# One tap later: moving the offset product, the last stages, a load, statistics and filter sums in a deformable bottleneck

## The chip, the cores and the metric

The kernel runs on one core of a Trainium2 chip. Its engines are TensorE (PE for products, PEld for the loading of its weights), VectorE (DVE), ScalarE (ACT), GpSimd (POOL) and SyncE (SP, which here only issues DMAs); each has a queue of its own that it works through in order. The metric is the time of one execution in microseconds (us); lower is better.

## The reference

Two bottleneck layers follow each other on x of shape (4, 1024, 56, 56), in float32.

Layer 0 is a deformable bottleneck: `r = relu(conv1x1(x, w1))` to 256 channels; `off = conv3x3(r, w_off)` to 18 channels, a (dy, dx) for each of nine taps; for each tap and pixel r is sampled bilinearly at the displaced position (four corners, weighted, zero outside the image); the nine samples go through the 256 by 256 weights of their taps and a relu; then `x1 = relu(x + conv1x1(r2, w3))` with 1024 channels.

Layer 1 is an ordinary bottleneck with batch normalisation: conv1x1 to 256 channels (y1), bn and relu, conv3x3 (y2), bn and relu, conv1x1 back to 1024 channels, bn, a scale by softplus(residual_scale), and `relu(x1 + ...)`. Each bn needs mean and variance over all four images, so each convolution has to be finished before its normalisation can begin.

## The kernel before

An image has 3136 pixels. They are cut in seven blocks j = 0..6 of 448 pixels for the first stage, and in seven of 512, 512, 512, 512, 384, 384 and 320 for the later ones, so 28 blocks (n, j) in all. Layer 0 and the first convolution of layer 1 run in one long loop.

**Stage a** (`stage_a`, one block): the 1x1 convolution 1024 to 256 (products L317, relu L309), the transposes of its result (`ftp`, L370, in two PSUM banks) and their copies on ACT (`ft`, L377, L379, L380), from which four DMAs write the sampling table in HBM (L384, L388); then the product for the offsets (`pm`, L396, in a bank of the same pool of two), its copy on ACT (`part`, L405, one buffer) and six small DMAs to `offc` (L413). Inside it `stage_b` works out the positions of the block two before. x is loaded by `load_x` (L266), two blocks ahead for image 0, one block ahead for the others.

**Taps.** For each block and each of nine taps `sample` gathers four corners (POOL's indirect DMA L480; first corner on ACT L490, the others added on DVE L492), `turn` transposes the samples (`stp` on PE L517, in the same pool of two banks; `sts` copied on ACT L523, sums on DVE L525 to L527), and `tap` multiplies (PE L545; seven products as in Strassen's scheme). After tap 8 the partial products are copied (ACT L560 to L564), added (DVE L566 to L572) and go through the relu to `r` (ACT L574). `sample` runs two taps ahead of `tap`, and `turn` one.

**Stage c** (`stage_c`, one block): for each of eight parts of channels, x is copied to a bank of `psz` (`pr`, ACT L597; x loaded as `xr`, SP L590), the product with w3 is added (L601), relu to `x1t` (ACT L612), store (L613); these feed the first convolution of layer 1 (`acc3`, L627, banks of the same `psz`, of which there are two). At its end the sum is copied to `y` (ACT L637), `bn_stats` is taken of that copy (DVE L639), and the copy is stored (SP L640).

```python
                nc.scalar.copy(y1s[h], z)
                if part == 1:
                    nc.vector.bn_stats(y1_stats[:, h, b * 6 : b * 6 + 6], y1s[h])
                    nc.sync.dma_start(y1_v[n, :, h, blk], y1s[h])
```

**The order** is written by hand: the loop over taps (L789 to L837) gives the stages a budget of work after each tap and takes them forward with `next()`. What a stage yields is its cost. A `None` ends the stage's share for this tap, so that what follows it in the stage comes after the next tap. `last_ones` holds the blocks whose taps are done and for which stage c may begin. Image 0's stages a are run before the loop. `filters` (L673 and the lines after it) prepares the filters of the second convolution in between, from the last image's second block on.

**After the loop** come the scale and shift of bn1 (`scale_shift`, L840: `bn_aggr` on DVE, square root on ACT L128, four small operations on DVE); the second convolution in Winograd's form (normalisation on ACT L910, transformed inputs on DVE L940 to L959, products L993, filter sums `us` on DVE L1129, outputs and statistics in `end`, L1032 to L1080); bn2; a phase that forms the moments of the normalised y2 (relu L1238, mean row `first` L1248, transposes `tp` L1208, products L1227), from which bn3 is had without running the last convolution twice; and the last convolution with the residual (L1334 on).

Of the kernel before, what the change touches and what calls it, by code (L numbers as in the profile page):

```python
# [61 lines left out]
def deform_bottleneck_then_bn_bottleneck(  # L62
# [25 lines left out]
    x1_v = x1_d.rearrange("n (k p) q -> n p k q", p=128)  # L88
    u0_d = dram.tile([128, KB * 3 * CB], F32, tag="u0_d", name="u0_d")
# [11 lines left out]
    nc.sync.dma_start(ch, chan)  # L101
# [11 lines left out]
    y1_stats = const.tile([128, KB, NB * 6], F32, tag="y1_stats", name="y1_stats")  # L113

    y2_stats = const.tile([128, KB, 3 + 2 * 4 * 6], F32, tag="y2_stats", name="y2_stats")
# [26 lines left out]
    nc.sync.dma_start(s_t, res_scale.to_broadcast([128, 1]))  # L142
# [27 lines left out]
    with ExitStack() as l0:  # L170
# [16 lines left out]

        w1 = wa.tile([128, KC, CB], F32, tag="w1", name="w1")
# [66 lines left out]
        def load_x(n, j, kk):  # L255
            if n == N:
                return
            if (n, j) == (0, 0):
                nc.sync.dma_start(w1[:, kk : kk + 2], w1_v[:, kk : kk + 2])
            if n == 0:  # L260

                xt = gat.tile([128, 4 * CB], F32, tag="g", name=f"xt_{n}_{j}_{kk}")
                xt = xt[:, : 2 * BLK].rearrange("p (k q) -> p k q", k=2)
            else:
                xt = xin.tile([128, 2, BLK], F32, tag="xt", name=f"xt_{n}_{j}_{kk}")
            nc.sync.dma_start(xt, x_v[n, :, kk : kk + 2, j * BLK : (j + 1) * BLK])  # L266
            xts[n, j, kk] = xt
# [35 lines left out]
        def stage_a(n, j):  # L303
# [23 lines left out]
            if n == 0:  # L327

                sums = [
                    pst.tile([128, 512], F32, tag=f"tap{2 * (j % 2) + h}", name=f"acc1_{b}_{h}")[  # L330
                        :, :BLK
                    ]
                    for h in range(KB)
                ]
                for k in range(KC):
                    for h in range(KB):
                        product(h, k, sums[h], k == 0)
                    if k % 2 and j + 2 <= NJ:
                        load_x(*((0, j + 2) if j + 2 < NJ else (1, 0)), k - 1)
                    yield KB * BLK  # L340
                for h in range(KB):
                    clip(h, sums[h], col("a_b1", h))
            else:

                def channels(h):
                    z = psz.tile([128, 512], F32, tag="z", name=f"acc1_{b}_{h}")[:, :BLK]
                    begin_with(z, col("a_b1", h))
                    yield
                    for k in range(KC):
                        product(h, k, z, False)  # L350
                        if k % 2:
                            if h == KB - 1:
                                load_x(*following, k - 1)
                            yield 2 * BLK
                    clip(h, z, 0.0)

                yield from run([channels(h) for h in range(KB)])
# [24 lines left out]
            for corner, s in enumerate((0, PW)):  # L382
                r = q - s + TPAD
                nc.sync.dma_start(  # L384
                    tables[n][r : r + QFULL * 128, corner, :].rearrange("(t p) c -> p t c", p=128),
                    ft[:, :QFULL, :],
                )
                nc.sync.dma_start(  # L388
                    tables[n][r + QFULL * 128 : r + QB, corner, :], ft[:QREST, QFULL, :]
                )  # L390

# [187 lines left out]
        def stage_c(n, j):  # L579
# [35 lines left out]
            def first(h, part):  # L615
                z = psz.tile([128, 512], F32, tag="z", name=f"acc3_{b}_{h}_{part}")[:, :size]
                if part == 0:
                    y1s.append(
                        w3p.tile([128, 512], F32, tag="y1", name=f"y1_{b}_{h}", bufs=2)[:, :size]
                    )  # L620
                    begin_with(z, col("b1", h))
                else:
                    nc.scalar.copy(z, y1s[h])
                yield
                for i in range(KC // 2):
# [9 lines left out]
                    if i % 2:  # L635
                        yield 2 * size
                nc.scalar.copy(y1s[h], z)  # L637
                if part == 1:
                    nc.vector.bn_stats(y1_stats[:, h, b * 6 : b * 6 + 6], y1s[h])  # L639
                    nc.sync.dma_start(y1_v[n, :, h, blk], y1s[h])  # L640
# [9 lines left out]
            yield from run(jobs)  # L650

# [4 lines left out]
        def filters():  # L656
# [36 lines left out]
            nc.sync.dma_start(u0_d, w_0)  # L693
            yield
# [93 lines left out]
        stage, upcoming, extra, budget = None, None, None, 0.0  # L788
        for i, (n, j, k) in enumerate(taps):  # L789
# [6 lines left out]
            if k == TAPS - 1:  # L796
                last_ones.append((n, j))
# [47 lines left out]
    with l1:  # L845
# [187 lines left out]
        def end(i, p, q):  # L1033

            n, half = parts[i]
            even, odd = halves(i, p)
            if p in WIN:
# [15 lines left out]
            def stats(k):  # L1053
                if i in ENDS:
                    for o in range(KB):
                        at = 3 + (ENDS.index(i) * 4 + k) * 6
                        nc.vector.bn_stats(y2_stats[:, o, at : at + 6], r[k][:, o])
# [4 lines left out]
            elif p == 4:  # L1062
# [62 lines left out]
        for ps in ((1, 2), (3, 4), (0,), (5,)):  # L1125
            inputs(0, ds[0], ps)
            for p in ps:
                if p not in WIN:
                    nc.vector.tensor_add(us[p], u[p][:, :, 0], u[p][:, :, 1])  # L1129
                elif p not in EARLY:  # L1130
# [37 lines left out]
    def sums_of_filters():  # L1168
        nc.vector.tensor_add(c3s[:, 0], quarter[:, 1, 0], quarter[:, 1, 1])
        nc.vector.tensor_sub(c3s[:, 1], c3s[:, 0], quarter[:, 0, 0])  # L1170
        nc.vector.tensor_sub(c3s[:, 2], quarter[:, 0, 0], quarter[:, 1, 0])
        nc.vector.tensor_sub(c3s[:, 3], quarter[:, 0, 1], c3s[:, 1])
# [26 lines left out]
    with ExitStack() as l2:  # L1199
# [47 lines left out]
        for h in range(KB):  # L1247
            nc.tensor.matmul(  # L1248
                first[:, h * 128 : (h + 1) * 128],
                ref[:, h : h + 1].to_broadcast([128, 128]),  # L1250
                ident,
                start=True,
                stop=True,
            )
# [4 lines left out]
        for i in range(0, len(chunks), 2):  # L1259
# [4 lines left out]
            tp, yt = pixels(i)  # L1264
# [263 lines left out]
```

## Time and profile before

| what | us |
|---|---|
| median of 3 runs | 2837.42 (2833.97 to 2839.52) |
| profiled execution | 2845.98 |
| its span, first to last instruction | 2844.2 |
| PE busy | 2740.3 (96%) |
| DVE busy | 2141.3 (75%) |
| ACT busy | 1487.6 (52%) |
| POOL busy | 1216.8 (43%) |
| mean granted clock of TensorE | 0.989 |

By the timeline, image 0's stages a run to about 135 us, the loop over taps to 2109, the second convolution to 2423, the moments to 2555 and the last convolution to the end. On the page, "busy" is the time in which an engine works on an instruction; in an answer of the timeline each row has the start, the busy time, engine, line, operation, output and inputs, and in brackets the idle time of the engine just before it, with what ended it. "acc<-sts,w" is a product of `sts` with the weights w; the names leave buffer numbers out.

### The profile page before, as it was taken

The numbers are of one execution on the slowest core, as the hardware profiler recorded it, in microseconds if no ns is written. First come the engines' busy times: TensorE is split into PE (matmuls) and PEld (weight loads), VectorE is DVE, ScalarE is ACT, GpSimd is POOL, SyncE is SP. The second block draws the span as 40 slices with busy tenths as digits, with TensorE's granted clock in tenths as the row PEclk, the third lists the DMA queues.
The fourth block names the chain that finished last, engine by engine and source line by source line (L and its number), as shares of the span: only waits on it lengthen the run. The fifth ranks groups of instructions, "written<-read, shape, count | busy, mean of one in ns | idle before, by whom it ended". The sixth has DMA issues, their size and how long they took to land.

```text
span 2844.2 us, 39220 instructions
## 1 busy us (share of the span) xinstructions
PE 2740.3 (96%) x11901; PEld 1903.5 (67%) x11901; DVE 2141.3 (75%) x5069; ACT 1487.6 (52%) x3007; POOL 1216.8 (43%) x1050
## 2 busy tenths in 40 slices
PE   9979999999999999999999989999989999999999
PEld 4445566676666676667676657666769999875454
DVE  2287777888787888778778988778849987437777
ACT  2245554665655556555565656666652554514444
POOL 0065666466666556656555665554500000011211
PEclk9999999999999999999999999999999999999999
DMA  8598898999999998999998989999930110209998
GB/s 275 182 348 324 323 338 308 343 321 345 336 331 349 352 316 309 335 340 335 341 342 284 352 302 358 352 342 332 311 131 24 49 35 12 93 29 345 349 344 303
DMA packets 313029, 792.16 MB, mean 279 GB/s; under 512 B 33737, under 2 KB 134641, under 8 KB 312817
## 3 DMA queue, kind: packets, MB, share of 16 engines
q0 software_dynamic: 127296, 462.48, 45.6%
q1 hardware_dynamic: 167088, 275.78, 28.3%
q10 hardware_dynamic: 18432, 51.39, 4.6%
q8 instruction: 94, 1.54, 0.2%
q14 instruction: 119, 0.97, 0.1%
HBM read 640.68 MB, written 143.48 MB: 276 GB/s over the span
## 4 chain that ended last, share of the span: by engine, by line
PE 82%; DMA 8%; DVE 3%; ACT 3%; issue 2%; SPq 1%; another core or an unknown queue 1%; POOL 0%; ACTq 0%; POOLq 0%; DVEq 0%
PE acc L545 19%; PE pr L601 11%; PE acc L627 11%; PE acc L317 10%; PE q L993 8%; PE stp L517 6%; DMA g<-table,idxs 5%; PE u L1409 4%; PE c L1409 2%; PE v L1409 2%; PE acc_g L1227 2%; PE pm L396 2%; PE b L993 2%; DVE s L492 2%; PE tp L1208 1%
## 5 line engine op out<-in xcount | busy, mean ns | idle before, releaser
L480 POOL DMA_INDIRECT g<-table,idxs x900 | 1148.1, 1276 | 914.6 <-DVE s L492 259.6
L492 DVE SCALAR_TENSOR_TENSOR s<-g,wts,s 128x256 f32<-128x256 f32 (+1 forms) x2700 | 1173.2, 480 | 321.5 <-ACT s L490 176.7
L545 PE MATMUL acc<-sts,w 128*128 128x256 f32 (+2 forms) x3528 | 725.0, 355 | 5.9 <-ACT sts L523 4.3
L545 PEld LDWEIGHTS acc<-sts,w 128*128 128x128 f32 x3528 | 602.9, 191 | 55.3 <-ACT sts L523 6.6
L490 ACT ACTIVATE s<-g,wts 128x256 f32<-128x256 f32 x900 | 425.5, 511 | 245.5 <-PE stp L517 109.8
L601 PE MATMUL pr<-r,w 128*128 128x512 f32 (+2 forms) x896 | 369.8, 551 | 16.0 <-ACT pr L597 8.0
L317 PE MATMUL acc<-xt,w 128*128 128x448 f32 x896 | 358.4, 543 | 9.4 <-DMA xt<-in_x_dram 8.6
L627 PE MATMUL acc<-x1t,c1w 128*128 128x512 f32 (+2 forms) x896 | 357.4, 540 | 3.6 <-ACT x1t L612 1.7
L517 PEld LDWEIGHTS stp<-ident,s 128*128 128x128 f32 (+1 forms) x1800 | 211.6, 141 | 145.9 <-issue 92.5
L601 PEld LDWEIGHTS pr<-r,w 128*128 128x128 f32 x896 | 165.7, 192 | 165.1 <-issue 94.2
L517 PE MATMUL stp<-ident,s 128*128 128x128 f32 (+1 forms) x1800 | 253.6, 274 | 20.6 <-DVE s L492 10.4
L317 PEld LDWEIGHTS acc<-xt,w 128*128 128x128 f32 x896 | 166.9, 191 | 147.8 <-issue 142.5
L627 PEld LDWEIGHTS acc<-x1t,c1w 128*128 128x128 f32 x896 | 167.5, 190 | 143.2 <-issue 92.6
L523 ACT COPY sts<-stp 128x512 f32<-128x512 f32 (+2 forms) x504 | 242.9, 530 | 33.0 <-PE stp L517 26.1
L612 ACT ACTIVATE x1t<-pr,ch 128x512 f32<-128x512 f32 (+2 forms) x224 | 141.9, 633 | 141.5 <-PE pr L601 125.3
L1360 ACT ACTIVATE x1f<-x1f,sh_bn 128x896 f32<-128x896 f32 x112 | 116.0, 1041 | 150.4 <-DVE x1f L1357 121.8
L637 ACT COPY y<-acc 128x512 f32<-128x512 f32 (+2 forms) x112 | 59.5, 531 | 200.5 <-PE acc L627 182.5
L527 DVE TENSOR_TENSOR sts<-sts 128x512 f32<-128x512 f32 (+2 forms) x252 | 155.9, 619 | 0.7
L597 ACT COPY pr<-xr 128x512 f32<-128x512 f32 (+2 forms) x224 | 121.4, 542 | 4.1
L1357 DVE SCALAR_TENSOR_TENSOR x1f<-u,sc_bn,x1f 128x448 f32<-128x448 f32 x156 | 106.6, 684 | 18.9 <-PE u L1409 9.4
L993 PE MATMUL q<-v,u 128*128 128x196 f32 x576 | 109.6, 337 | 9.9 <-DVE v L945 8.7
L525 DVE TENSOR_TENSOR sts<-sts 128x256 f32<-128x256 f32 (+2 forms) x252 | 97.4, 387 | 25.4 <-ACT sts L523 21.3
(246 smaller groups left out, 2858.2 us busy)
## 6 DMA issues: line engine op xcount, KB each, us to landing
xt<-in_x_dram SPq DMA_DIRECT2D x112, 448.0 KB
x1f<-x_d SPq DMA_DIRECT2D x96, 448.0 KB
out_dram<-x1f ACTq DMA_DIRECT2D x96, 448.0 KB
xr<-in_x_dram SPq DMA_DIRECT2D x128, 256.0 KB
x_d<-x1t SPq DMA_DIRECT2D x128, 256.0 KB
table<-ft SPq DMA_DIRECT2D x56, 384.0 KB
g<-table,idxs POOLq DMA_INDIRECT x900
xr<-in_x_dram SPq DMA_DIRECT2D x64, 192.0 KB
```

The costliest lines, as they stand in the source:

```text
L317: nc.tensor.matmul(acc, w1[:, k, h * 128 : (h + 1) * 128], xts[n, j, k - k % 2][:, k % 2, :], start=start, stop=(k == KC - 1), skip_group_ ...
L480: nc.gpsimd.indirect_dma_start(out=g[:m], out_offset=None, in_=tables[n].rearrange("r q c -> r (q c)"), in_offset=bass.IndirectOffsetOnAxi ...
L490: nc.scalar.activation(s[:m], g[:m, 0:CB], AF.Copy, scale=wt[:, 0])
L492: nc.vector.scalar_tensor_tensor(s[:m], g[:m, corner * CB : (corner + 1) * CB], wt[:, corner], s[:m], ALU.mult, ALU.add,)
L517: nc.tensor.transpose(banks[h][:, t * 128 : t * 128 + m], s[:m, h * 128 : (h + 1) * 128], ident[:m, :m],)
L523: nc.scalar.copy(to, banks[h][:, :size].rearrange("p (e q) -> p e q", e=2))
L527: nc.vector.tensor_sub(sts[:, 5:7, :half], sts[:, 1:4:2, :half], sts[:, 0:2, :half])
L545: nc.tensor.matmul(sums[i], w2[:, a, k], sts[:, b, :half], start=(k == 0 and i % 2 == 0), stop=(k == TAPS - 1), skip_group_check=True,)
L601: nc.tensor.matmul(z, w3[:, h, k * 128 : (k + 1) * 128], r2[:, h, :size], start=False, stop=(h == KB - 1), skip_group_check=True,)
L627: nc.tensor.matmul(z, c1w[:, k, h * 128 : (h + 1) * 128], x1ts[k], start=False, stop=(i == KC // 2 - 1), skip_group_check=True,)
L993: nc.tensor.matmul(ps[:, o].rearrange("p r c -> p (r c)"), wt, x, start=first and j == 0 and (alone or o == 0), stop=last and j == len(pai ...
L1409: nc.tensor.matmul(to, wt, x, start=start, stop=stop, skip_group_check=True)
```

## The change

- The loads of `ch` and `s_t` are issued on ACT's queue instead of SP's.
- In `stage_a` a `yield None` stands ahead of the offset product, which then comes a tap later.
- A block enters `last_ones` one tap later than before (`done`).
- x block (1, 1) is loaded within stage a of (0, 6), into tiles of the pool of `r2` that are idle then.
- `bn_stats` of y1 reads the PSUM bank, ahead of the copy; y1 lies in tiles of another pool.
- `statistics` aggregates all blocks but the last ahead of the end; the last aggregate merges the result with the last block's (`y1_ends`).
- `filters` also forms three sums of filters (us1, us3, and us0, which is stored to HBM and loaded back).
- In the last part of the second convolution far_t is added to the halves before the last products (`closing`), statistics 1 and 2 come later, and the last statistics are of each half.
- The four sums of the last filters are formed on POOL instead of DVE.
- The mean row is multiplied between the first transposes of the moments phase.

```diff
-    nc.sync.dma_start(ch, chan)
+    nc.scalar.dma_start(ch, chan)
-    nc.sync.dma_start(s_t, res_scale.to_broadcast([128, 1]))
+    nc.scalar.dma_start(s_t, res_scale.to_broadcast([128, 1]))
+        y1_t = [wp.tile([128, 512], F32, tag=f"y1_{h}", name=f"y1_{h}") for h in range(KB)]
...
+            elif (n, j) == (1, 1):
+
+                xt = work.tile([128, KB, 512], F32, tag="r2", name=f"xt_{n}_{j}_{kk}", bufs=R2S)
+                xt = xt[:, :, :BLK]
...
-                    if k % 2 and j + 2 <= NJ:
-                        load_x(*((0, j + 2) if j + 2 < NJ else (1, 0)), k - 1)
+                    if k % 2:
+                        load_x(*((0, j + 2) if j + 2 < NJ else (1, j + 2 - NJ)), k - 1)
...
-                            if h == KB - 1:
+                            if h == KB - 1 and following != (1, 1):
...
+            yield None
+
             pm = ps1.tile([128, BLK], F32, tag="bank", name=f"pm_{b}")
...
-                    y1s.append(
-                        w3p.tile([128, 512], F32, tag="y1", name=f"y1_{b}_{h}", bufs=2)[:, :size]
-                    )
+                    y1s.append(y1_t[h][:, :size])
...
+                if part == 1:
+                    at = b * 6 if b < NB - 1 else 3
+                    to = y1_stats if b < NB - 1 else y1_ends
+                    nc.vector.bn_stats(to[:, h, at : at + 6], z)
                 nc.scalar.copy(y1s[h], z)
                 if part == 1:
-                    nc.vector.bn_stats(y1_stats[:, h, b * 6 : b * 6 + 6], y1s[h])
                     nc.sync.dma_start(y1_v[n, :, h, blk], y1s[h])
...
+        def statistics():
+
+            mv = const.tile([128, KB, 2], F32, tag="mv_y1", name="mv_y1")
+            count = float(N * HW - SIZES[-1])
+            for h in range(KB):
+                nc.vector.bn_aggr(mv[:, h, :], y1_stats[:, h])
+            nc.vector.memset(y1_ends[:, :, 0], count)
+            nc.vector.tensor_copy(y1_ends[:, :, 1], mv[:, :, 0])
+            nc.vector.tensor_scalar_mul(y1_ends[:, :, 2], mv[:, :, 1], count)
...
+            us_0 = w3p.tile([128, 512], F32, tag="x1t", name="us_0", bufs=X1S)
+            w_00 = w_0.rearrange("p (h j o) -> p h j o", h=KB, j=3)
+            nc.vector.tensor_add(
+                us_0.rearrange("p (h o) -> p h o", h=KB), w_00[:, :, 0], w_00[:, :, 1]
+            )
+            nc.sync.dma_start(us0_d, us_0)
...
+            for p in (1, 3):
+                us[p] = pool.tile([128, KB, CB], F32, tag=f"us{p}", name=f"us{p}")
+                nc.vector.tensor_add(us[p], u[p][:, :, 0], u[p][:, :, 1])
+                yield
...
             tap(n, j, k)
-            if k == TAPS - 1:
-                last_ones.append((n, j))
+            if done is not None:
+                last_ones.append(done)
+            done = (n, j) if k == TAPS - 1 else None
...
-            if extra and k in (1, 4, 7):
+            if extra and k in (1, 3, 5, 7):
...
+        last_ones.append(done)
         while last_ones or stage or upcoming:
             if stage is None:
+                if upcoming is None and len(last_ones) == 1:
+                    statistics()
...
+            if upcoming and not last_ones:
+                statistics()
...
-    sc1, sh1 = scale_shift(y1_stats, KB, cols("g1", KB), cols("be1", KB), "bn1")
+    sc1, sh1 = scale_shift(y1_ends, KB, cols("g1", KB), cols("be1", KB), "bn1")
...
+        nc.sync.dma_start(us[0], us0_d.rearrange("p (h o) -> p h o", h=KB))
...
+            closing = (i, p) == (len(parts) - 1, SEQ[-1])
+            if closing:
+                for to, c in ((odd, 1), (even, 0)):
+                    nc.vector.tensor_add(to, to, far_t[..., c:W:2])
...
-                stats(1)
-                stats(2)
+                if i == 0:
+                    stats(1)
+                    stats(2)
             elif p == 0:
                 nc.vector.tensor_add(r[0], r[0], sum_t)
                 stats(0)
+                if i:
+                    stats(1)
+                    stats(2)
+            elif closing:
+                stats(3, even)
+                stats(3, odd, 1)
...
-                if p not in WIN:
-                    nc.vector.tensor_add(us[p], u[p][:, :, 0], u[p][:, :, 1])
-                elif p not in EARLY:
+                if p in WIN and p not in EARLY:
...
-        nc.vector.tensor_add(c3s[:, 0], quarter[:, 1, 0], quarter[:, 1, 1])
+        nc.gpsimd.tensor_add(c3s[:, 0], quarter[:, 1, 0], quarter[:, 1, 1])
...
-        def pixels(i):
+        def pixels(i, between=None):
...
+                if c == 0 and between is not None:
+                    between()
...
-            tp, yt = pixels(i)
+            tp, yt = pixels(i, mean_row if i == 0 else None)
```

More of the change, by code (lines that the diff above doesn't have):

```diff
@@ L88, in deform_bottleneck_then_bn_bottleneck @@
     x1_v = x1_d.rearrange("n (k p) q -> n p k q", p=128)
+    us0_d = dram.tile([128, KB * CB], F32, tag="us0_d", name="us0_d")
     u0_d = dram.tile([128, KB * 3 * CB], F32, tag="u0_d", name="u0_d")
@@ L112, in deform_bottleneck_then_bn_bottleneck @@
     nc.vector.memset(eps_t, EPS)
-    y1_stats = const.tile([128, KB, NB * 6], F32, tag="y1_stats", name="y1_stats")
-    y2_stats = const.tile([128, KB, 3 + 2 * 4 * 6], F32, tag="y2_stats", name="y2_stats")
+    y1_stats = const.tile([128, KB, (NB - 1) * 6], F32, tag="y1_stats", name="y1_stats")
+    y1_ends = const.tile([128, KB, 3 + 6], F32, tag="y1_ends", name="y1_ends")
+    y2_stats = const.tile([128, KB, 3 + (2 * 4 + 1) * 6], F32, tag="y2_stats", name="y2_stats")
     def scale_shift(stats, k, g, be, name):
@@ L787, in deform_bottleneck_then_bn_bottleneck @@
         turn(*taps[0])
-        stage, upcoming, extra, budget = None, None, None, 0.0
+        stage, upcoming, extra, done, budget = None, None, None, None, 0.0
         for i, (n, j, k) in enumerate(taps):
@@ L1051, in end, with stats @@
             r = [rows_of(n, half, k) for k in range(4)]
-            def stats(k):
+            def stats(k, of=None, more=0):
                 if i in ENDS:
+                    of = r[k] if of is None else of
                     for o in range(KB):
-                        at = 3 + (ENDS.index(i) * 4 + k) * 6
-                        nc.vector.bn_stats(y2_stats[:, o, at : at + 6], r[k][:, o])
+                        at = 3 + (ENDS.index(i) * 4 + k + more) * 6
+                        nc.vector.bn_stats(y2_stats[:, o, at : at + 6], of[:, o])
             if p == 2:
@@ L1168, in sums_of_filters @@
     def sums_of_filters():
-        nc.vector.tensor_add(c3s[:, 0], quarter[:, 1, 0], quarter[:, 1, 1])
-        nc.vector.tensor_sub(c3s[:, 1], c3s[:, 0], quarter[:, 0, 0])
-        nc.vector.tensor_sub(c3s[:, 2], quarter[:, 0, 0], quarter[:, 1, 0])
-        nc.vector.tensor_sub(c3s[:, 3], quarter[:, 0, 1], c3s[:, 1])
+        nc.gpsimd.tensor_add(c3s[:, 0], quarter[:, 1, 0], quarter[:, 1, 1])
+        nc.gpsimd.tensor_sub(c3s[:, 1], c3s[:, 0], quarter[:, 0, 0])
+        nc.gpsimd.tensor_sub(c3s[:, 2], quarter[:, 0, 0], quarter[:, 1, 0])
+        nc.gpsimd.tensor_sub(c3s[:, 3], quarter[:, 0, 1], c3s[:, 1])
     def wide(n, j, k, name):
@@ L1246, in deform_bottleneck_then_bn_bottleneck, with mean_row @@
         first = ps1.tile([128, 512], F32, tag="bank", name="first")
[L1247 to L1254, printed above, removed]
+        def mean_row():
+            for h in range(KB):
+                nc.tensor.matmul(
+                    first[:, h * 128 : (h + 1) * 128],
+                    ref[:, h : h + 1].to_broadcast([128, 128]),
+                    ident,
+                    start=True,
+                    stop=True,
+                )
         relu(0, 128, BLK)
```

## The prediction

> **What bounds the kernel now.** I read the page's busy shares first, then the timeline of TensorE (PE) in stretches, its gaps, and what ScalarE (ACT), VectorE (DVE) and the DMA queues did in each.
>
> ```profile
> PE 2740.3 (96%) x11901; PEld 1903.5 (67%) x11901; DVE 2141.3 (75%) x5069; ACT 1487.6 (52%) x3007; POOL 1216.8 (43%) x1050
> ```
>
> TensorE is idle for 2844.2 − 2740.3 = 104 us only. The change removes no matmul, so what it can win is some of those 104 us, and the half-clock time behind them. In the record of the granted clock every gap of about 2 us and more is followed by 3.4, 6.8 or 10.2 us at 0.5; 6.8 us at half speed are 3.4 us of lost work. Three places matter. The first is stage c of block 2, on the timeline of PE and of ACT:
>
> ```profile
> 310.88 0.60 PE L545 MATMUL acc<-sts,w 128*128 128x256 f32 x2
> 316.32 2.93 PE L601 MATMUL pr<-r,w 128*128 128x512 f32 x3 [4.84 <-ACT r L574]
> ...
> 312.51 0.51 ACT L490 ACTIVATE s<-g,wts 128x256 f32<-128x256 f32 x1 [2.72 <-DMA g<-table,idxs]
> 315.56 1.32 ACT L574 ACTIVATE r<-r,ch 128x512 f32<-128x512 f32 x2
> ```
>
> The reader sees stage c's first product wait for the relu of r, which stands on ACT behind samples that wait for gathers. The second is the offset product, here of block 14:
>
> ```profile
> 696.39 1.04 PE L370 MATMUL ftp<-ident,feat 128*128 128x128 f32 x8
> 697.27 0.70 PE L601 MATMUL pr<-r,w 128*128 128x320 f32 x2
> 700.03 2.31 PE L396 MATMUL pm<-feat,woff 128*64 128x448 f32 x6 [2.06 <-ACT ft L377]
> ...
> 699.00 0.51 ACT L490 ACTIVATE s<-g,wts 128x256 f32<-128x256 f32 x1 [1.53 <-DMA g<-table,idxs]
> 699.41 0.57 ACT L377 COPY ft<-ftp 128x512 f32<-128x512 f32 x1
> ```
>
> Ten such gaps (1.00, 0.61, 0.42, 2.06, 1.31, 0.71, 0.38, 1.85, 0.93, 0.83) sum to 10.1 us. The third is the boundary to the second convolution, and its end:
>
> ```profile
> 2109.06 0.43 PE L627 MATMUL acc<-x1t,c1w 128*128 128x320 f32 x1
> 2109.59 0.43 ACT L637 COPY y<-acc 128x320 f32<-128x320 f32 x1 [1.78 <-PE acc L627]
> 2110.03 1.28 ACT L128 ACT_TABLE_LOAD   x1
> 2110.04 0.33 SPq L640 DMA_DIRECT2D y_d<-y  x1
> 2110.57 0.91 DVE L121 BATCH_NORM_AGGREGATE mv_bn<-y_stats 128x2 f32<-128x168 f32 x1
> 2112.70 4.12 ACT L910 ACTIVATE y<-rows,sh_bn,sc_bn 128x812 f32<-128x812 f32 x4 [0.88 <-DVE sh_bn L133]
> 2114.70 1.29 DVE L1129 TENSOR_TENSOR us<-u 128x512 f32<-128x512 f32 x2 [2.10 <-DMA y_d<-y]
> 2118.01 0.67 PE L993 MATMUL q<-v,u 128*128 128x196 f32 x1 [8.51 <-DVE v L945]
> ...
> 2421.14 1.63 PE L993 MATMUL q<-v,u 128*128 128x196 f32 x8 [0.59 <-ACT y L1031]
> 2425.37 0.61 DVE L121 BATCH_NORM_AGGREGATE mv_bn<-y_stats 128x2 f32<-128x51 f32 x2
> 2427.14 7.19 ACT L1238 ACTIVATE y<-y,sh_bn,sc_bn 128x128 f32<-128x128 f32 x12 [0.82 <-DVE sh_bn L133]
> 2428.77 1.20 PE L1248 MATMUL first<-ident,both 128*128 128x128 f32 x4 [6.00 <-issue]
> ```
>
> At the first, a chain of statistics; DVE waits until 2114.70 for the last store (4.6 us after issue). At the second, PE waits 6.00 us behind statistics, aggregate and first relu.
>
> **The Trainium skill.** "TensorE: Matmul & The Clock Gate", Part 1, gives half clock after an idle window of about 3.4 us; the trace agrees on the half, though gaps from 2 us can bring it. "PSUM — Partial Sum Buffer", bank collisions, has two engines on one bank ordered, two readers too. So in the new order the copy of z on ACT must wait for the statistics that DVE reads from z; before, the copy (0.43 to 0.59 us) went first and statistics read its result. The same page's section on engine and sequencer instructions says that ACT's and DVE's queues are strict FIFO: what stands behind a waiting copy waits too (the ft copy above did). "DMA: Bandwidth & Descriptors", anatomy of one DMA, puts about 2 us on a DMA's completion; here 4.6 us, and that is used.
>
> **The change part by part**, against the profiled execution (span 2844.2, time 2845.98 us; the median of the runs is 2837.42, 8.6 lower).
>
> *Two small loads to ACT's queue.* SP issued ch and s_t at 0.74 and 1.19, w at 1.65 us. The first product (6.45 us) waits for x; x moves up by 0.9 us, and PE is full until 104 us: −0.9.
>
> *Offset product a tap later.* The order of PE after the change has the transposes ftp, one or two products, then stp of the next tap, which needs the same two banks and so the same ft copy. Pm's 10.1 us do not vanish, they stand before stp. Taken 0; −10 if ACT's copies come earlier, +4 since stp loses pm's 2.5 us of cover for DVE's samples (blocks 17 and 24 had them 2.6 and 1.5 us after the copy). The part copy moves too: at 215.38 stp waited 5.45 us for it (then 6.8 at half clock, 8.9 in all), since the previous block's six offc DMAs filled its buffer. Both blocks shift alike and stp still follows: −1.5, between −8.9 and 0. Those offc DMAs pass to a later place of SP's queue, behind the tap's other loads and stores; their readers, the positions, run two blocks later and have tens of microseconds.
>
> *Stage c a tap later.* The products of one more tap stand before it, and the relu is done by then: 4.84 + 3.4 = 8.2 us at 311. Stage c's xr loads and x1 stores on SP shift with it, in step with their consumers. DVE's samples are late there as well, so −7 (0 if stp waits in its place). The same wait at 2087.82 (2.57) stays: the last tile's order is unchanged.
>
> *x block (1,1) ahead.* 1.8 MB go into image 0's stages, where PE is full and DMA half free; the 1.3 MB of xr that stood there go later. At 155.67 PE waited 2.14 us for this x, and in the stretch 137 to 235 PE is busy for 75.9 of 98 us while the DMA engines are at 0.92 and 335 GB/s. The net 0.5 MB less in that stretch is 1.5 us; the wait is 2.1 more. One may contain the other: −2.5, between −6 and +2 (xr late for stage c of block 0 after 240 us).
>
> *Statistics from PSUM.* 56 statistics of 0.48 to 0.71 us now stand between the last product and the copy. The bank comes free 0.8 to 1.2 us later (DVE's own work ahead included; 4 to 10 in four cases near 1118 to 1130 and 1672 to 1680). Of the two banks' slack, counted block by block in the trace before, two cases had 0.1 us or less, two 1.2 and 1.6, all others 2.3 or more. That is 1 to 3 us; ACT held behind adds little while it is at 52%. +2.5, between 0 and +25.
>
> *Boundary.* The early aggregate saves part of 0.91 us, but the square root cannot start before the table load ends at 2111.31 (it started at 2111.52). The two adds of 1.29 leave DVE. Against this y copy comes 0.5 us later, and y1's new place is memory that the normalised image takes: the first normalisation waits for the store, 2110.5 + 4.6 = 2115.2 instead of 2112.70. It then gives the first 1.03 us piece at 2116.2 and a second at 2117.3, where L940 began at 2115.91: +1, between −2 and +3, at half clock all the same.
>
> *Filters.* Three adds of 0.65 us on DVE, hidden in its 25% (the edges' adds before 2116 are what they replace), and 262 KB out and back, 0.8 us each at 340 GB/s. On SP the store stands ahead of the rows load, read only at the boundary some 400 us on, and the reload ahead of the u loads, which waited for the store's landing at 2114.69 in any case: +0.5; +3 if uncovered. The 5.24 us gap at 1647, DVE waiting on the end filters, stays.
>
> *End of the second convolution.* The two statistics moved off DVE before 2417 are replaced there by one subtraction of like length: the gap of 2.71 stays. After the last product DVE had 0.56 + 0.98 + 1.04 us to the aggregate; now 0.56 + 0.56 and four half statistics: −0.5. The transposes start with the first two relus, about 0.6 and 1.1 us after 2426.6, mean row between them: −1.2. The four sums on POOL free 2.7 us of DVE where PE waits 0.26 at most: 0; POOL's memsets behind them have three buffers of lead, +1 otherwise.
>
> Sum: −0.9 + 0 − 1.5 − 7 − 2.5 + 2.5 + 1 + 0.5 − 0.5 − 1.2 = −9.6. The profiled execution would be at 2836.4; a timed run at 2837.4 − 9.6 = 2827.8, say **2828**.
>
> **Rivals.** (A) The sum as above, 2818 to 2836; chance 0.50. (B) Pm's waits fall as well, since the ft copies lie ahead of the samples once the tap is re-spaced, and with them 215: −9.6 − 10.1 − 7.4 = −27, 2810; for it speaks that PE has no other work due in these gaps, against it the order; 0.20. (C) The gaps only move: stp waits at 311 for late samples, and x fills no gap: −9.6 + 7 + 2.5 = 0, some 2837; 0.15. (D) Slower: the copy's wait on DVE. ACT, FIFO, holds samples and sts copies behind each of 56 copies; with 0.45 us of each exposed, 25 us, in place of 2.5: −9.6 − 2.5 + 25 = +13, 2850. It decides past 0.32 us exposed a time (56 times that are 18 us, against −12.1, 5.7 above no change). For it: DVE has some 6.5 us of work in a tap of 7.3 and takes its samples from ACT. Against it: two banks with slack over 2 us. 0.15.
>
> **How the numbers follow.** 0.2% is 5.7 us, about what a measurement tells from no change. Faster (under 2831.7): 0.8 of A, all of B, a little of C: 0.62. Same: 0.2 of A, most of C: 0.23. Slower: D, 0.15. B's tail and the milder half of D give the range 2805 to 2845; A's own is 2818 to 2836.
>
> **What would show it.** Right: no gap at 311, first product near 5.5 us, ten small gaps now before stp with ft L385 as releaser, ACT's y copy released by DVE, the boundary gap at 9 to 10, the one at 2422 at about 4.5. Wrong: new ACT-bound gaps in the loop after stage c's ends; a pm group without waits and nothing in its place; a boundary under 8.

## The result, and the profile after

The changed kernel takes 2864.68 us (median of 8 runs, 2851.31 to 2880.35) where the kernel before takes 2838.47 in the same comparison (8 runs, 2832.65 to 2845.91): the ratio is 1.0092, 95% interval 1.0068 to 1.0117. That is 26 us slower. 2828 us and a gain were forecast. The two profiled executions lie closer together, their spans 21 us apart, so what the traces show below is somewhat less than the loss.

The page after, busy shares, then the costliest groups of PE that wait, with their idle time and its first releaser:

```profile
span 2865.3 us, 39151 instructions
...
PE 2754.3 (96%) x11901; PEld 1906.3 (67%) x11901; DVE 2139.3 (75%) x5073; ACT 1491.4 (52%) x3007; POOL 1227.5 (43%) x1054
...
L611 PE MATMUL pr<-r,w 128*128 128x512 f32 (+2 forms) x896 | 371.1, 556 | 20.4 <-ACT pr L607 13.3
L527 PE MATMUL stp<-ident,s 128*128 128x128 f32 (+1 forms) x1800 | 261.8, 275 | 39.8 <-ACT ft L385 14.7
```

The same two groups on the page of the kernel before:

```profile
L601 PE MATMUL pr<-r,w 128*128 128x512 f32 (+2 forms) x896 | 369.8, 551 | 16.0 <-ACT pr L597 8.0
L517 PE MATMUL stp<-ident,s 128*128 128x128 f32 (+1 forms) x1800 | 253.6, 274 | 20.6 <-DVE s L492 10.4
```

The number of matmuls is the same, 11901. PE's idle time went from 2844.2 − 2740.3 = 104 us to 2865.3 − 2754.3 = 111, and 14 us more are "busy": the time at half clock went from 67.2 to 79.9 us, which is some 6 of the 14, and the rest lies, it seems, in the steps between matmuls, which are pipelined with modelled ends, so that a short wait counts as busy. By stage, from the starts and ends of the same products in both traces (the first stretch ends at the start of PE's first gap of over 1 us after it has begun, 2.83 us before and 3.27 after, ahead of transposes of image 0):

| stretch | before, us | after, us | difference |
|---|---|---|---|
| start to that gap | 104.28 | 105.77 | +1.5 |
| from there to the end of the loop | 2005.2 | 2021.3 | +16.0 |
| boundary to the second convolution | 8.51 | 9.39 | +0.9 |
| second convolution | 304.8 | 306.9 | +2.2 |
| gap at its end | 6.00 | 4.42 | −1.6 |
| the rest, to the last product | 410.1 | 412.2 | +2.2 |

So most of the loss sits in the loop over taps. The 2.2 us of the second convolution and of the rest were not followed up. The waits of the loop, on the timeline of PE and of ACT; first at the place of the 4.84 us gap, then a wait of stp behind ftp:

```profile
309.25 3.60 PE L611 MATMUL pr<-r,w 128*128 128x512 f32 x8
317.00 3.78 PE L611 MATMUL pr<-r,w 128*128 128x512 f32 x4 [4.16 <-ACT pr L607]
...
313.82 0.51 ACT L500 ACTIVATE s<-g,wts 128x256 f32<-128x256 f32 x1 [2.83 <-DMA g<-table,idxs]
315.96 0.51 ACT L500 ACTIVATE s<-g,wts 128x256 f32<-128x256 f32 x1 [1.05 <-DMA g<-table,idxs]
316.37 0.58 ACT L607 COPY pr<-xr 128x512 f32<-128x512 f32 x1
...
880.87 1.04 PE L378 MATMUL ftp<-ident,feat 128*128 128x128 f32 x8
881.75 1.03 PE L555 MATMUL acc<-sts,w 128*128 128x256 f32 x4
885.14 0.55 PE L527 MATMUL stp<-ident,s 128*128 128x128 f32 x3 [2.36 <-ACT ft L385]
```

Stage c now starts without waiting for the relu, and stops four products later (each leaves two records, hence x8) for the copy of x: ACT is held by samples that wait for gathers either way. And stp waits for the copies of ft, as pm did before.

The boundary, and the end of the second convolution:

```profile
2127.05 0.50 DVE L648 BATCH_NORM_STATS2 y_ends<-acc 128x6 f32<-128x320 f32 x1 [1.42 <-PE acc L635]
2127.64 0.42 ACT L649 COPY y<-acc 128x320 f32<-128x320 f32 x1 [1.78 <-DVE y_ends L648]
2129.38 0.29 ACT L131 ACTIVATE sc_bn<-mv_bn,eps_t 128x2 f32<-128x2 f32 x1
2132.18 4.14 ACT L948 ACTIVATE y<-rows,sh_bn,sc_bn 128x812 f32<-128x812 f32 x4 [2.50 <-DMA y_d<-y]
2136.41 0.99 PE L1031 MATMUL q<-v,u 128*128 128x196 f32 x2 [9.39 <-issue]
...
2445.40 0.67 DVE L124 BATCH_NORM_AGGREGATE mv_bn<-y_stats 128x2 f32<-128x57 f32 x2
2447.76 1.41 PE L1256 MATMUL tp<-ident,y 128*128 128x128 f32 x3 [4.42 <-ACT y L1288]
```

Shift and scale are ready at 2130.46 (the last of their operations on DVE), 3.4 us after the last product, but the normalisation starts 1.7 us later, at 2132.18, released by the store of y, whose memory its result takes. In brackets is ACT's whole idle time, 2.50.

### The profile page after: what moved, and what is told of

Same layout as the page of the kernel before. It is cut to its first block, busy times and chain, and to the rows that moved or that the text cites. A ratio compares the mean times of both kernels' runs of the same rounds, so it can differ in the third digit from the quotient of the medians.

```text
span 2865.3 us, 39151 instructions
## 1 busy us (share of the span) xinstructions
PE 2754.3 (96%) x11901; PEld 1906.3 (67%) x11901; DVE 2139.3 (75%) x5073; ACT 1491.4 (52%) x3007; POOL 1227.5 (43%) x1054
## 4 chain that ended last, share of the span: by engine, by line
PE 63%; DMA 7%; DVE 4%; ACT 3%; issue 2%; ACTq 0%; SPq 0%; POOLq 0%; POOL 0%; DVEq 0%
PE acc L555 14%; PE pr L611 9%; PE acc L635 9%; PE q L1031 7%; PE acc L325 5%; PE stp L527 4%; DMA g<-table,idxs 4%; PE u L1462 3%; PE acc_g L1277 2%; PE c L1462 2%; PE b L1031 2%; PE v L1462 2%; DVE s L502 2%; DMA out_dram<-x1f 1%; PE pm L406 1%
## 5 line engine op out<-in xcount | busy, mean ns | idle before, releaser
L555 PE MATMUL acc<-sts,w 128*128 128x256 f32 (+2 forms) x3528 | 732.9, 356 | 1.2 <-issue 0.6
L527 PE MATMUL stp<-ident,s 128*128 128x128 f32 (+1 forms) x1800 | 261.8, 275 | 39.8 <-ACT ft L385 14.7
```

The source lines that it names most:

```text
L527: nc.tensor.transpose(banks[h][:, t * 128 : t * 128 + m], s[:m, h * 128 : (h + 1) * 128], ident[:m, :m],)
L555: nc.tensor.matmul(sums[i], w2[:, a, k], sts[:, b, :half], start=(k == 0 and i % 2 == 0), stop=(k == TAPS - 1), skip_group_check=True,)
```

## The experiments

A ratio is to the kernel before on the same chip, with its 95% interval. Kernels named together in one heading, unless it says otherwise, ran on one chip; across headings only the ratios compare. The intervals reach 0.001 to 0.003 to each side; a difference that they cover tells nothing.

### Undoing one of three parts, and all three

Three parts of the change act on the loop: the pause ahead of the offset product (P), stage c a tap later (C), the statistics read from PSUM ahead of the copy (B). Each is undone in the changed kernel.

`u_pm`, P undone:

```diff
-            yield None
-
             pm = ps1.tile([128, BLK], F32, tag="bank", name=f"pm_{b}")
```

> The changed kernel with the offset product back at its old place (no yield ahead of it), all else as changed. Theory P, the offset product: its wait went to stp and grew there (stp stalls +27 us, pm stalls -12 in the loop), so most of the loop's loss goes: 12 to 16 us faster than the changed kernel, ratio to before about 1.004. Theory B, the copy that waits for the statistics: this run stays near 1.009, within 4 us of the changed kernel. Theory C, the later stage c: the same, near 1.009.

`u_bn`, B undone:

```diff
+                nc.scalar.copy(y1s[h], z)
                 if part == 1:
...
-                    nc.vector.bn_stats(to[:, h, at : at + 6], z)
-                nc.scalar.copy(y1s[h], z)
+                    nc.vector.bn_stats(to[:, h, at : at + 6], y1s[h])
```

> The changed kernel with the statistics of y1 taken of the copy again, after it; all else as changed. Theory B: ACT waited 82 us for DVE in 27 of these copies, and this held the samples back; without it 10 to 15 us faster than the changed kernel, ratio to before about 1.004 to 1.005. Theory P or C: not over 3 us faster, near 1.008 to 1.009.

`u_c`, C undone for all blocks but the last:

```diff
-            if done is not None:
-                last_ones.append(done)
-            done = (n, j) if k == TAPS - 1 else None
+            if k == TAPS - 1 and i + 1 < len(taps):
+                last_ones.append((n, j))
```

> The changed kernel with a block's stage c free to begin right after its tap 8 again (for all blocks but the last, whose order is the same anyway). Theory C: the copies of x for stage c now meet the samples that wait for gathers (pr stalls of 4.2 us at 313 and 3.3 at 402); undone, 5 to 10 us faster than the changed kernel, ratio about 1.006. Theory P or B: within 3 us of the changed kernel, or slower by up to 8 us, since the gap of 4.84 us at 311 and its half clock come back.

`u_all3`, the three edits together:

> The changed kernel with all three of these undone: what is left is the early x block, the earlier loads, statistics(), the filter sums and the end of the second convolution. If the three carry the loss, this is 3 to 8 us faster than before (ratio 0.997 to 0.999). If it stays at 1.004 or more, the loss lies in the rest: the early x block or the queues it shifts.

| kernel | ratio | interval |
|---|---|---|
| changed | 1.0092 | 1.0068 to 1.0117 |
| u_pm | 1.0039 | 1.0026 to 1.0052 |
| u_bn | 1.0069 | 1.0050 to 1.0089 |
| u_c | 1.0050 | 1.0031 to 1.0069 |
| u_all3 | 0.9994 | 0.9978 to 1.0009 |

The three together carry the loss: 0.0098 of it, 28 us, go when they are undone. The rest of the change is worth nothing that these runs can tell, where 3 to 8 us had been expected. Undoing P gives 15 us; undoing C gives 12, where the theory P or B had expected 3 at most (the two intervals just touch); B's 6.5 us fit neither of its expectations, lie within the two intervals and show nothing yet.

### One part alone, and both transposes and product late

From `u_all3`, one part is put back. `r_pm` has P alone, `r_c` C alone, `r_bn` B alone. `r_both` moves the transposes a tap later too, so that pm follows ftp directly as before:

```diff
             yield None
+            yield None
 
             ft = worka.tile([128, QFULL + 1, CB], F32, tag="ft", name=f"ft_{b}")
```

> From the kernel with all three undone (ratio 0.9994), the offset product alone moved a tap later again. Theory P: it costs by itself what its undoing gave, 12 to 15 us (ratio 1.004 to 1.005). If the three need each other (a rival: each loss is only there in company), under 5 us, ratio below 1.001.

> As r_pm, but the transposes ftp are moved a tap later together with the offset product, so that pm still follows ftp directly and stp does not. Theory P in its narrow form (the loss comes from stp standing right behind ftp, in whose banks it waits for the copies of ft, not from lateness): ratio within 0.0015 of 0.9994. Rival, lateness of the stage itself: as r_pm, 1.004 or more.

> From the kernel with all three undone, stage c alone a tap later again. Theory C: 5 to 12 us slower than 0.9994, ratio 1.001 to 1.004. The forecast of the prediction (the gap of 4.84 us at 311 and its half clock go): 3 to 8 us faster, 0.997 to 0.998.

> From the kernel with all three undone, the statistics alone taken from PSUM ahead of the copy. Theory B: 4 to 8 us slower, ratio 1.001 to 1.002. If the undoing's 0.0023 was noise: within 2 us of 0.9994.

| kernel | ratio | interval |
|---|---|---|
| r_pm | 1.0034 | 1.0020 to 1.0049 |
| r_both | 1.0169 | 1.0144 to 1.0194 |
| r_c | 1.0009 | 0.9997 to 1.0022 |
| r_bn | 1.0002 | 0.9988 to 1.0017 |

P costs 0.0040, 11 us, alone. C alone costs 0.0015, some 4 us, with intervals that overlap, and B alone nothing that shows (2 us, where 4 to 8 had been expected). Alone the three make some 17 us by these figures, together 28: part of the loss seems to come only in company, the rival that `r_pm` was to tell from theory P. `r_both` felled the narrow theory: with pm directly behind ftp again it is not near 0.9994 but 50 us slower than `u_all3`, far beyond the 1.004 named for mere lateness, which it does not rule out. What waits for what (the list of waits by tile, with the sum in us and the number of waits: for stp in `r_pm`, then for pm in `u_all3`, then for pm in `r_both`) shows where the wait for the copies stands:

```profile
  DVE s L502: 12.1, 11
  ACT ft L385: 11.1, 7
```

```profile
  ACT ft L385: 10.8, 10
```

```profile
  ACT ft L386: 26.5, 15
```

The wait for the copies of ft is 11.1 us at stp in `r_pm` and 10.8 at pm in `u_all3`. There it moved and did not grow, and the 11 us that P costs must come on top, which the narrow theory does not explain. In `r_both` it grew, at its old place.

What `r_pm` and `r_both` have in common is the pause itself. A `None` ends the stage's share of this tap with its budget unspent; the budget is carried over. I counted in the trace, for the taps of 512 pixels, the products that PE has from one tap to the next, each at its usual step. The idea: a short tap lets PE run ahead of the samples, which ACT and DVE can't hurry; the unspent work comes in a later, long tap:

| kernel | taps under 7 us | over 12 us | ratio |
|---|---|---|---|
| u_all3 | 26 | 6 | 0.9994 |
| r_pm | 34 | 11 | 1.0034 |
| r_both | 35 | 11 | 1.0169 |

(DVE's work in such a tap is some 6.5 us. Another choice of the usual step moves these counts by two to four taps; that a pause adds short and long ones stays.) The theory formed from this, S: the pause costs because it cuts the share. The counts don't give the size of the loss: `r_pm` and `r_both` have nearly the same and lose 11 and 50 us. In the traces of `u_all3`, `r_pm` and `r_both` PE is idle for 61.3, 70.4 and 90.5 us of the loop, and works at half clock for 29.7, 34.9 and 67.2.

### The share kept, and the share cut without reordering

`r_fill` is `r_pm` with the pause mended: the next stage, which has begun by then, takes the rest of the share; the paused stage is finished after the next tap.

```diff
-            yield None
+            yield LATE
...
             budget += share * SIZES[j]
+            if held is not None:
+                for cost in held:
+                    budget -= cost or 0
+                held = None
...
+                elif cost == LATE:
+                    if not due(n, j, k):
+                        if upcoming is None:
+                            break
+                        held, stage, upcoming = stage, upcoming, None
```

> As r_pm (offset product a tap later, the other two undone), but where the stage pauses ahead of the offset product the next stage, already begun, takes the rest of the tap's share; the paused one is finished after the next tap. Theory S, the cut share: r_pm loses because its pause ends the share with budget unspent, so that PE has only the tap's own 4.3 us of products there (23 such taps of under 5 us against 16) and then waits for samples. Then this one is back at 0.9994 or below, 0.995 to 1.000, and the pauses of pm for the copies of ft (10.8 us) are gone too. Rival L, lateness of the offset product itself (its copy, its DMAs, the positions): as r_pm, 1.003 or more.

`r_cut` leaves pm where it was and cuts a share elsewhere, in stage a's convolution:

```diff
                             yield 2 * BLK
+                        if k == 3 and h == KB - 1:
+                            yield None
```

> From the kernel with all three undone, one more pause in the middle of stage a's convolution, in each block of images 1 to 3; nothing is reordered around ftp, pm or stp, only the share of one more tap is cut short. Theory S: it costs like r_pm, 6 to 15 us, ratio 1.0015 to 1.005. Rival L, or the place of stp behind ftp: within 3 us of 0.9994.

`r_sp` is `u_all3`, and `f_sp` is `r_fill`, with the two small loads on SP's queue again:

```diff
-    nc.scalar.dma_start(ch, chan)
+    nc.sync.dma_start(ch, chan)
...
-    nc.scalar.dma_start(s_t, res_scale.to_broadcast([128, 1]))
+    nc.sync.dma_start(s_t, res_scale.to_broadcast([128, 1]))
```

> From the kernel with all three undone, the two small loads back on SP's queue. The prediction had the move at -0.9 us; the traces with it have the first product at 6.8 to 7.9 us instead of 6.45. If the queue is the cause: first product near 6.5 us, 0.4 to 1.3 us faster, ratio 0.9990 to 0.9993, which the timing can hardly tell; the trace can. If that was only scatter of the first transfers, the first product comes at 7 us here as well.

> r_fill with the two small loads back on SP's queue. Theory S: 0.995 to 1.000 and equal to r_fill within 2 us. Rival L: 1.003 or more.

| kernel | ratio | interval | taps under 7 us | over 12 us |
|---|---|---|---|---|
| r_fill | 0.9981 | 0.9964 to 0.9999 | 26 | 6 |
| f_sp | 0.9974 | 0.9961 to 0.9988 | 27 | 6 |
| r_cut | 1.0086 | 1.0054 to 1.0118 | 35 | 9 |
| r_sp | 0.9988 | 0.9966 to 1.0010 | | |

Both tests answer for S, and `r_fill` rules out rival L for the offset product: with the share kept it is still a tap late, and 0.0053 (15 us) of `r_pm`'s ratio are gone. With one more share cut and the order around ftp, pm and stp as before, 0.0092 (26 us) are lost, more than the 15 us at most that I expected. The waits of stp in `r_fill`:

```profile
  DVE s L502: 13.6, 8
  ACT off L453: 5.9, 5
  issue: 1.9, 3
  ACT ft L385: 1.5, 2
```

In 16 of the 21 blocks four to ten products of stage c now stand between ftp and stp, and the wait for ft is 1.5 us where `r_pm` had 11.1. In `r_cut` pm waits for it nearly twice as long as in `u_all3`; this line is of pm's waits in `r_cut`:

```profile
  ACT ft L387: 21.4, 7
```

So the tests leave open by which waits the cut costs. Stp's waits for samples, of which S had spoken, did not fall with the share kept (12.1 us in `r_pm`, 13.6 in `r_fill`); the wait for ft did, by 9.6 us. And the pause of `r_cut` also puts off what follows it in stage a, the transposes among it; no run had these late with the share kept and nothing else changed.

The start, in the kernel before and in the changed one:

```profile
2.12 0.47 SPq L266 DMA_DIRECT2D xt<-in_x_dram  x1
6.45 1.83 PE L317 MATMUL acc<-xt,w 128*128 128x448 f32 x2 [6.45 <-DMA xt<-in_x_dram]
...
1.25 0.47 SPq L274 DMA_DIRECT2D xt<-in_x_dram  x1
7.78 1.09 PE L325 MATMUL acc<-xt,w 128*128 128x448 f32 x1 [7.78 <-DMA xt<-in_x_dram]
```

`r_sp` and `f_sp` have their first product at 6.57 and 6.75 us. In the eight kernels with the loads on SP that are run here it lies between 6.41 and 6.75, in the eleven with them on ACT (the changed kernel's 7.78 among them) between 6.68 and 7.91. The issue of x is 0.87 us earlier with them on ACT's queue (1.25 instead of 2.12 us), and x lands later all the same. The time of a run shows none of this (`r_sp` against `u_all3`, `f_sp` against `r_fill`). Why x lands later was not tried.

### The later stage c and the statistics, with the pause mended

`f_c` is `f_sp` with C; `f_c1` the same for images 1 to 3 only; `f_cb` is `f_c` with B; `f2` is `f_sp` with the older pause, ahead of ftp, mended in the same way (`yield LATE`). These four share a chip.

```diff
+            done = None
+            if k == TAPS - 1 and i + 1 < len(taps):
+                if n:
+                    done = (n, j)
+                else:
+                    last_ones.append((n, j))
```

(The diff is what `f_c1` has and `f_c` has not.)

> f_sp (ratio 0.9974) with stage c a tap later. If the later stage c costs by itself, because its copies of x then stand behind samples that wait for gathers: 4 to 12 us slower, 0.9988 to 1.0016. If its loss came only together with the cut share: within 3 us of f_sp.

> f_c with image 0's blocks left as in f_sp; stage c is a tap later for images 1 to 3 alone. If the loss sits in the first blocks, where gathers are behind (the traces with the later stage c fall back between 300 and 470 us): within 3 us of f_sp. If it is spread over all blocks: like f_c.

> f_c with the statistics taken from PSUM ahead of the copy: the whole change, but for the two small loads and with the pause mended. If the statistics cost 2 to 6 us here too: 0.001 to 0.002 above f_c. If not: within 0.0015 of it. In both cases well below the 1.0092 of the change as made.

> f_sp with the older pause, ahead of the transposes ftp, also giving the rest of its share to the next stage. Theory S: a further 3 to 10 us, ratio 0.994 to 0.9965. If only the new pause hurt: 0.997 to 0.998, within 2 us of f_sp.

| kernel | ratio | interval |
|---|---|---|
| f_c | 0.9993 | 0.9979 to 1.0007 |
| f_c1 | 0.9977 | 0.9967 to 0.9986 |
| f_cb | 1.0023 | 1.0013 to 1.0034 |
| f2 | 0.9960 | 0.9945 to 0.9975 |

C stands 0.0019 over `f_sp` (5 us), which ran on the chip of the heading before and whose interval it overlaps, and 0.0003 when image 0 is spared. So its loss points to the first blocks; the intervals of `f_c` and `f_c1` overlap by a little too, and the place is likely, not settled. The gaps agree: between 225 and 480 us `f_c` has PE waits over 1 us of 2.43, 3.00, 1.18 and 4.87 us, `f_c1` 1.70, 1.38 and 3.74, and `f_sp` 1.62, 1.93 and 2.14.

B costs 0.0030, 8.5 us, more than the 2 to 6 us expected, and here the intervals stand apart. In the lists of waits (us in all, times, longest) of the changed kernel and of `f_cb`, ACT's copy waits for DVE:

```profile
ACT y L649 <- DVE y_stats L648: 81.8, 27, 4.5
```

```profile
ACT y L649 <- DVE y_stats L648: 84.7, 29, 4.3
```

In `f_cb` it waits 84.7 us in 29 places, up to 4.3 us at a time; in `f_c` this copy waits for PE alone. The statistics stand behind DVE's samples, which wait for ACT's, and ACT now waits for the statistics. That ACT's wait is what costs is not shown by this.

`f2`, with the older pause mended too, is 0.0014 (4 us) below `f_sp`: in the direction and of the size that S gave, but within the intervals, so that the older pause cost as well is likely, not shown. It has 19 taps under 7 us, and 3 over 12.

### How the statistics cost, and the early x block

`f_bz` is `f_c` with the statistics read from the bank but after the copy. `f2_nox` is `f2` without the early x block.

```diff
                 nc.scalar.copy(y1s[h], z)
...
-                    nc.vector.bn_stats(to[:, h, at : at + 6], y1s[h])
+                    nc.vector.bn_stats(to[:, h, at : at + 6], z)
```

> f_c (0.9993) with the statistics taken from the PSUM bank, but after ACT's copy instead of ahead of it: DVE waits for ACT as before the change, the bank is held for copy and statistics as after it. If the loss of f_cb is ACT held behind DVE: within 0.0015 of f_c. If it is the bank that comes free later: like f_cb, 1.001 to 1.0035.

```diff
-            elif (n, j) == (1, 1):
-
-                xt = work.tile([128, KB, 512], F32, tag="r2", name=f"xt_{n}_{j}_{kk}", bufs=R2S)
-                xt = xt[:, :, :BLK]
...
-                    if k % 2:
-                        load_x(*((0, j + 2) if j + 2 < NJ else (1, j + 2 - NJ)), k - 1)
+                    if k % 2 and j + 2 <= NJ:
+                        load_x(*((0, j + 2) if j + 2 < NJ else (1, 0)), k - 1)
...
-                            if h == KB - 1 and following != (1, 1):
+                            if h == KB - 1:
```

> f2 (0.9960) without the early x block: block (1, 1) is loaded one block ahead again. By the prediction's step (-2.5 us, -6 to +2) this is 2.5 us slower, ratio 0.9969, which is at the edge of what the timing tells; 0.998 or more if the block's place matters more than that, 0.996 or less if it gains nothing. In the trace a wait of 1 to 3 us for x returns near 150.

`f_bz` came to 1.0008 (0.9987 to 1.0029), between `f_c` and `f_cb` and apart from neither. Whether B costs by holding ACT or by holding the bank stays open. `f2_nox` came to 0.9935 (0.9913 to 0.9957): the early x block has no gain that shows; `f2` on another chip had 0.9960, and the intervals overlap. A wait of 1.60 us for x stands at 156.96 in its trace, as expected, and doesn't decide the time. `f2_nox`, with a median of 2829.24 us against 2846.41 of the kernel before beside it, has the lowest ratio of this study: with both pauses mended, and C, B, the two small loads and the early x block undone, what is left of the change is 0.65% faster than the kernel before. `f2` is not told apart from it.

## Why the prediction was wrong

**The step that failed is "Offset product a tap later", taken 0, between −10 and +4.** Its mechanism was half right: the waits do stand before stp, with ft L385 as releaser, and their sum stayed (11.1 us for 10.8). Left out was that a `yield None` is not only a place in the order. It ends the stage's share of the tap, in 21 blocks, and makes some taps short and others long. I had read the loop that spends the budget and counted the instructions that the pause moves, and not the work that it takes away from the tap. The pause costs 11 us alone and 15 in the changed kernel; the loss goes when the share is kept (`r_fill`), and one more cut share brings a loss of 26 us (`r_cut`). By which waits a cut share costs stays open in part. That rival was not in the list. The −1.5 for the copy `part` can't be put down to this step: the wait of 5.45 us is gone in the changed kernel, but also in `u_all3`, where pm is not late.

**"Stage c a tap later", −7 between 0 and −8.2, had the wrong sign.** The relu is ready, as predicted, and PE begins; then it waits 4.16 us for the copy of x. The lines shown in the prediction had the reason in them, samples on ACT waiting for gathers. I took the instruction behind them for the cause, and the next instruction of ACT that PE needed, the copy of x, waited there in its place. The step measured +4 to +12, by the kernel around it, instead of −7; only the +12 is near clear of noise. Rival C had this right for 311 ("stp waits at 311"), though it is pr that waits.

**"Statistics from PSUM", +2.5 between 0 and +25.** The sign was right and the size too small: 8.5 us with the pause mended, 6.5 and 2 (not clear of noise) elsewhere. I had priced the bank's slack, and set ACT's holding to little because ACT is busy for 52%. ACT waited 82 us for these statistics in the changed kernel; which of the two costs is open (`f_bz`). Rival D put the loss on ACT's wait, with 25 us for it. Its total, 2850, lies on the right side by luck: these statistics are a smaller part of the loss, and the part that is largest was not in it.

**"Two small loads", −0.9:** the issue was earlier as worked out, the landing was not. The first product came 1.3 us later in the profiled execution.

**"x block ahead", −2.5:** PE's idle time from 135 to 226 us fell from 21.3 to 13.1 us, so waits there went, the one for x among them, but with the pauses mended `f2_nox` is no slower without it.

**Boundary, +1:** +0.9 by the trace, and by the chain foreseen, the normalisation behind the store. **End of the second convolution, −0.5 and −1.2:** 6.00 to 4.42, −1.6.

**The half clock.** The prediction says that every gap of about 2 us and more is followed by it. That was misread: in the trace before, gaps of 2.58 us (ending at 151.5), 2.14 (at 157.8) and 2.57 (at 2090.4) are not. The half clock can also begin within a gap, 1.7 us before the end of the one of 4.84, so that less was lost behind it than the 3.4 us taken: (6.8 − 1.7) / 2, some 2.6. PE's work at half clock grew from 5.4 to 8.7 us at the boundary, where I had left it as it was, and went from 8.5 to 7.9 at the end of the second convolution. The Trainium skill, "TensorE: Matmul & The Clock Gate", Part 1, has the window by which the clock is set free-running; the traces agree: at that end the changed kernel and all eighteen variants have the same two gaps, 2.73 and 4.42 us, and between 3.4 us (`u_bn`) and 17.1 us (`r_pm`) at half clock with them. What a gap of this size costs is to that extent chance.

As a sum: −0.9 + 0 − 1.5 − 7 − 2.5 + 2.5 = −9.4 stood for the loop and the start, and undoing the three parts P, C and B takes 28 us away. The range missed it because P's pause was priced at nothing, C with the wrong sign, and nothing was set down for what the parts seem to cost in company.

## What to carry to other kernels

Where stages are interleaved by a budget, look at each pause as a cut in the work of that stretch, and give the rest of the share to another stage: here that took 15 us off. When PE waits for an engine whose queue is held by a late input, moving PE's next step may only change which instruction of that queue it waits for, as at 311 and 317 us here; ask what holds the queue. An engine at half load, like ACT with 52% here, can still be the one that others wait for, if it works in order and has waits of its own.

## What the runs showed of the hardware that was not expected

The first transfers landed later with two small loads on a second queue: first product at 6.68 to 7.91 us in eleven traces, 6.41 to 6.75 in eight, and 6.45 in the kernel before, with the loads on SP ahead of x, though x was issued 0.87 us earlier.

In the twenty traces every stretch at half clock, but the one in which a trace ends, lasts 3.41 us or two to five times that (6.83, 10.24, 13.65, 17.07). The length of a gap alone doesn't tell whether one comes: in the kernel before, a gap of 2.06 us (ending at 700.0) was followed by 3.4 us of it, and one of 2.58 us (ending at 151.5) by none.
